# Down projection of a feed-forward block in seven block products over pairs of batches

## The chip, the cores and the metric

The kernel runs on one core of a Trainium2 chip. The metric is device time in microseconds (us). The times given for the kernel before are three runs of it; a profile is one further execution. All arithmetic is in float32.

In the text PE is the matrix engine, PEld its loading of the stationary operand, DVE the vector engine, ACT the scalar engine, POOL the GpSimd engine, and SP the engine that issues most of the transfers. A line such as L721 is a line of the kernel's source. The changed kernel is longer, so its lines are given with the statement they hold.

## The reference, cut to what matters

The input x has 8 batches of 128 tokens with 512 features. A cross attention with 32 heads of 128 comes first, then a feed-forward block (FFN) of 1376 inner features; each has a layer norm ahead of it and a residual around it.

```python
def ffn(x):                       # Wg, Wu: 1376 x 512; Wd: 512 x 1376
    gate = einsum('bsh,ih->bsi', x, Wg) * ag
    up   = einsum('bsh,ih->bsi', x, Wu) * au
    h    = silu(gate) * up        # 8 x 128 x 1376
    return einsum('bsi,hi->bsh', h, Wd) * ad    # ad: one factor for each of 512 outputs
x = x + xattn(layernorm(x), ctx, mask, ...)
x = x + ffn(layernorm(x))
```

The change concerns the last `einsum`, its factor `ad`, and the last sum. It also splits off the code that makes `h`.

## The kernel before

The contracted axis always lies on the 128 partitions. 1376 inner features make 11 slices (`NI`), the last with 96 rows. A float32 matmul of the program shows up as two matmul records, so a count of records is twice the count of products.

**Seven products.** Most of the projections multiply two-by-two blocks with seven block products for eight. Sums of blocks of one operand (`sums_a`: s1, s2, s4 and one in place) and of the other (`sums_b`: t1, t2, t4 and one in place) are made beforehand, and PSUM results are combined afterwards. `seven` drives one such group for the FFN: product 2, product 1, then 6, 7 and 4 accumulated on top of product 1's banks, and then 5 and 3. Between products, ACT copies a bank out (L236, L246) or DVE adds it to what is in SBUF (L241, L252). The matmul that accumulates on a bank waits until that copy has read it.

**The stages at the end.** (1) Attention output projection for a pair of batches `i` (L470), each followed by `residual` (L537), which adds the seven products to x1. Two of its additions run on POOL: L545 for the left half of one batch, and L548 for the right half. Their result is `x1[i]`. (2) `norm2` (L558) takes mean and variance of `x1[i]` on DVE (L148, L149), and scales it to `y` (L567). (3) `norm2_T` transposes `y` on PE (L153), and DVE and ACT copy the result into `h2` (L579, L580). For the last pair (i = 3) this has one PSUM bank, so the second batch's transposes wait until both copies of the first are done. (4) `last_slice(0)` multiplies the 96-row slice for the first 512 tokens (L655, names `gp` and `up`). These 512 tokens need nothing of pair 3. (5) Sums of token blocks, `T_h` (L668 to L671, one of them on POOL: L669). (6) Five iterations of the gate and up projection, two slices each (L690, name `mm_f`), with POOL making sums of weights (L194 to L197), and `gated` (L640 on ACT, L641 and L644 on DVE) turning two results into `act`. (7) The down projection (L721, name `dn`):

```python
for n, ic in enumerate([NI - 1, *range(NI - 1)]):
    nc.tensor.matmul(
        o, act[ic][:m, bass.ts(b, S)], wd[:m, ic, cols],
        start=(n == 0), stop=(n == NI - 1),
    )
nc.vector.tensor_tensor(r[:, cols], o, ad_sb[:, cols], ALU.mult)
nc.vector.tensor_tensor(r[:, cols], r[:, cols], x1[b // 2][:, b % 2, cols], ALU.add)
nc.sync.dma_start(out[b][:, cols], r[:, cols])
```

Batches 0 to 6 have 11 products of 512 columns, and batch 7 has 22 of 256 columns in two halves, so that only half of its result remains at the end. The weights `wd` are loaded on SP (L627, L629).

**Order.** The order of the instructions on each engine is settled when the program is built, and isn't quite that of the source. The build moves an instruction ahead of others that were written earlier where its operands seem due sooner. In the trace, for example, POOL makes the weight sums of the first FFN iteration (L194 to L197, from 925.47 us) before the additions L545 and L548 of pair 3 (932.33 and 934.98 us), which are written earlier. On the chip each engine then takes its instructions in that order, and each waits for what it needs.

**Buffers.** `work` holds small tiles by tag ("pb", "tt", "s", "aT", "pT"), and a new tile of a tag waits until the oldest tile of that tag is free. `acts` has 18 buffers of 4 KB a partition for `x1`, `h2`, `gate` and the like; `ps` has 7 PSUM banks with the tag "m", and one with the tag "tp".

Of the kernel before, what the change touches and what calls it, by code (L numbers as in the profile page):

```python
# [10 lines left out]
F32 = mybir.dt.float32  # L11
U8 = mybir.dt.uint8
AF = mybir.ActivationFunctionType
ALU = mybir.AluOpType
# [3 lines left out]
P = 128  # L18
# [8 lines left out]
def xattn_ffn_kernel(  # L27
# [19 lines left out]
    nc = tc.nc  # L47
    B, S, D = x.shape
    H = pbias.shape[0]
    INTER = wgT.shape[1]  # L50
    T = B * S
# [5 lines left out]
    NI = (INTER + P - 1) // P  # L57
# [3 lines left out]
    HW = GW // 2  # L61
    ADD, SUB = ALU.add, ALU.subtract

    def pools(stack):
        def pool(name, bufs=1, **kw):
            return stack.enter_context(tc.tile_pool(name=name, bufs=bufs, **kw))
        return pool

    pool = pools(ctx)
# [3 lines left out]
    acts = pool("acts", 18, reuse_waits="tile")  # L73
    work = pool("work", 2, side="right", reuse_waits="tile")
# [7 lines left out]
    ps_mm, ps_tp, ps = (pools(attn)(f"ps{n}", 2, space=PSUM) for n in ("mm", "tp", "at"))  # L82
# [55 lines left out]
    ad_sb = const.tile([P, D], F32, name="ad_sb")  # L138
# [53 lines left out]
    def sums_a(eng, a11, a12, a21, a22, s1, s2, s4):  # L192

        eng.tensor_tensor(s1, a21, a22, ADD)  # L194
        eng.tensor_tensor(s2, s1, a11, SUB)
        eng.tensor_tensor(a21, a11, a21, SUB)
        eng.tensor_tensor(s4, a12, s2, SUB)  # L197
        return {1: a11, 2: a12, 3: s4, 4: a22, 5: s1, 6: s2, 7: a21}
# [94 lines left out]
    def probabilities(g, b, qT, kT, pb):  # L293
        cols = bass.ts(b, S)
        n = f"{g}_{b}"
        s = work.tile([P, GH, S], F32, tag="s", name=f"s_{n}", bufs=3)
        nc.gpsimd.tensor_tensor(  # L297
            s, pb, mneg[:, b : b + 1, :].to_broadcast([P, GH, S]), ALU.add
        )
        sc = ps.tile([P, GH, S], F32, tag="sc", name=f"sc_{n}")  # L300
        for j in range(GH):
            nc.tensor.matmul(  # L302
                sc[:, j, :], qT[:, j, bass.ts(b % 2, S)], kT[j][:, cols], start=True, stop=True
            )
        nc.vector.tensor_tensor(s, sc, s, ALU.add)  # L305
        mx = small.tile([P, GH], F32, tag="mx", name=f"mx_{n}")
        nc.vector.tensor_reduce(mx, s, AX.X, ALU.max)
        nmx = small.tile([P, GH], F32, tag="nmx", name=f"nmx_{n}")
        nc.vector.tensor_scalar(nmx, mx, FLOOR, -1.0, ALU.max, ALU.mult)  # L309
        sm = small.tile([P, GH], F32, tag="sm", name=f"sm_{n}")  # L310
        for j in range(GH):
            nc.scalar.activation(  # L312
                s[:, j, :], s[:, j, :], AF.Exp,
                bias=nmx[:, j : j + 1], accum_out=sm[:, j : j + 1],
            )
        ri = small.tile([P, GH], F32, tag="ri", name=f"ri_{n}")
        nc.vector.tensor_scalar_max(ri, sm, TINY)
        nc.vector.reciprocal(ri, ri)
        nc.vector.tensor_tensor(
            s, s, ri.unsqueeze(2).to_broadcast([P, GH, S]), ALU.mult  # L320
        )
        return s
# [137 lines left out]
    def by_product(banks):  # L460
        return {n: banks[k // 2][:, k % 2, :] for k, n in enumerate((1, 2, 6, 7, 4, 5, 3))}
# [26 lines left out]
    todo = [(g, i) for g in range(NG) for i in range(B // 2)]  # L488
# [3 lines left out]
    for g in range(NG):  # L492
        kT, v = kvs.pop(g)
        pb = biases.pop(g)
# [16 lines left out]
        for b in range(B):  # L511
# [5 lines left out]
            p = probabilities(g, b, qT, kT, pb)  # L517
# [15 lines left out]
    ps = pool("psO", 7, space=PSUM, reuse_waits="tile")  # L533
# [48 lines left out]
    x1, ys, banks = [], [], first_banks  # L582
    for i in range(B // 2):
        last = i + 1 == B // 2
# [7 lines left out]
        m = by_product(banks)  # L592
        x1.append(acts.tile([P, 2, D], F32, tag="a", name=f"x1_{i}"))
        for k in range(2):
            b = 2 * i + k
# [11 lines left out]

    fw = pool("fw", 4, reuse_waits="tile")
    wdp = pool("wdp", reuse_waits="tile")
    actp = pool("act", NI, reuse_waits="tile")  # L610
    NP = NI // 2

    def load_gate_up(i, eng=nc.sync):
# [10 lines left out]
    def load_down():  # L624
        t = wdp.tile([P, NI, D], F32, tag="wd", name="wd")
        full = INTER // P
        nc.sync.dma_start(t[:, :full, :], wdT[: full * P, :].rearrange("(c p) n -> p c n", p=P))  # L627
        if INTER % P:
            nc.sync.dma_start(t[: INTER % P, full, :], wdT[full * P :, :])  # L629
        return t  # L630

    act = [actp.tile([P, T], F32, tag="act", name=f"act_{ic}") for ic in range(NI)]
    alone = load_gate_up(NP, nc.gpsimd)
    gate_up = [load_gate_up(0, nc.gpsimd)]
    residual(i, x1[i], m, banks)
    ys = norm2(i, x1[i])

    def gated(act, gate, up, ic, m, sg):

        nc.scalar.activation(sg, gate, AF.Sigmoid, scale=ag_sb[:m, ic : ic + 1])  # L640
        nc.vector.scalar_tensor_tensor(  # L641
            sg, gate, ag_sb[:m, ic : ic + 1], sg, ALU.mult, ALU.mult
        )
        nc.vector.scalar_tensor_tensor(  # L644
            act, up, au_sb[:m, ic : ic + 1], sg, ALU.mult, ALU.mult
        )

    def last_slice(th):

        ic, m = NI - 1, INTER - (NI - 1) * P  # L650
        o = []
        for w, nm in zip(alone, ("gp", "up")):
            o.append(ps.tile([P, 512], F32, tag="m", name=f"{nm}_{th}"))
            for c in range(DC):
                nc.tensor.matmul(  # L655
                    o[-1][:m], w[:, c, :m], h2[c // HC, th][:, c % HC, :],
                    start=(c == 0), stop=(c == DC - 1),
                )
        sg = work.tile([P, 512], F32, tag="pT", name=f"sg_{th}", bufs=4)
        gated(act[ic][:m, bass.ts(th, 512)], o[0][:m], o[1][:m], ic, m, sg[:m])  # L660

    last_slice(0)
    for y in ys:
        norm2_T(*y)
    t1, t2, t3, t4 = (
        acts.tile([P, HC, 512], F32, tag="a", name=f"T{n}_h2") for n in range(1, 5)
    )
# [7 lines left out]
    for i in range(NP):  # L675
        ws, gate = [], [acts.tile([P, T], F32, tag="a", name=f"gate_{i}_{r}") for r in range(2)]
        for nm, w in zip("gu", gate_up[i]):
            s = fw.tile([P, 3, HC, P], F32, tag="S", name=f"S_{nm}{i}")
            ws.append(sums_a(
                nc.gpsimd, w[:, :HC, :P], w[:, HC:, :P], w[:, :HC, P:], w[:, HC:, P:],  # L680
                s[:, 0], s[:, 1], s[:, 2],
            ))
        if i + 1 < NP:
            gate_up.append(load_gate_up(i + 1))
        if i == 0:
            wd = load_down()

        def product(n, t, out, first):
            for c in range(HC):
                nc.tensor.matmul(  # L690
                    out, ws[t][n][:, c, :], h2_t[n][:, c, :],
                    start=(first and c == 0), stop=(c == HC - 1), skip_group_check=True,
                )

        def part(r, c, t):
            return (gate[r - 1], act[2 * i + r - 1])[t][:, bass.ts(c - 1, 512)]

        for n, _ in enumerate(seven(f"f{i}", range(2), product, part, ps, "m")):
            if i == 0 and n == 3:
                last_slice(1)  # L700
            if 4 <= n < 12 and n % 2 == 0 and gatings:
                gatings.pop(0)()
        for r in range(2):
            ic = 2 * i + r
            sg = acts.tile([P, T], F32, tag="a", name=f"sg_{ic}")
            for cols in (bass.ts(0, 512), bass.ts(1, 512)):
                gatings.append(partial(
                    gated, act[ic][:, cols], gate[r][:, cols], act[ic][:, cols], ic, P, sg[:, cols]
                ))
    for gating in gatings:  # L710
        gating()

    for b in range(B):
        r = work.tile([P, D], F32, tag="aT", name=f"r_{b}")
        parts = 1 if b + 1 < B else 2
        for k in range(parts):
            cols = bass.ts(k, D // parts)
            o = ps.tile([P, D // parts], F32, tag="m", name=f"dn_{b}_{k}")
            for n, ic in enumerate([NI - 1, *range(NI - 1)]):
                m = min(P, INTER - ic * P)  # L720
                nc.tensor.matmul(  # L721
                    o, act[ic][:m, bass.ts(b, S)], wd[:m, ic, cols],
                    start=(n == 0), stop=(n == NI - 1),
                )
            nc.vector.tensor_tensor(r[:, cols], o, ad_sb[:, cols], ALU.mult)
            nc.vector.tensor_tensor(r[:, cols], r[:, cols], x1[b // 2][:, b % 2, cols], ALU.add)
            nc.sync.dma_start(out[b][:, cols], r[:, cols])


# [41 lines left out]
```

## Time and profile before

| what | value |
|---|---|
| three runs | 1152.23 us median, 1151.07 to 1153.02 |
| the profiled execution, its own time | 1152.01 us |
| its span in the trace | 1150.2 us, so 1.8 us lie around the span |
| mean granted clock of PE | 0.991 |
| PE busy | 1120.0 us, 97% of the span |
| DVE, ACT, POOL busy | 502.3, 318.1, 297.9 us |
| end of attention output projection | 934.2 us from the start of the span |
| FFN gate and up | 934.2 to 1070.7 us |
| down projection on PE | 1070.7 to 1146.5 us |
| last DVE instruction to end of span (the last store) | 1147.4 to 1150.2 us |

The profile has one row for a group of instructions with the same line, engine and shapes. It gives the count, the busy time of the group, the mean duration of one in ns, and the idle time of the engine just before them with what ended it. Matmuls overlap, so their mean duration is longer than their spacing; spacing comes from busy time over count. The timeline lists instructions in order of time with start and length; runs of the same kind are merged.

### The profile page before, as it was taken

Reading aid. Unit: us, or ns where it says so; the run is one execution under the profiler, and the core shown is the slowest. Engines: PE = TensorE matmul, PEld = TensorE weight load, DVE = VectorE, ACT = ScalarE, POOL = GpSimd, SP = SyncE. Lnnn points to the kernel's source line nnn. Section 1 sums busy time; section 2 is a strip of 40 time slices with the busy share of each in tenths; the row PEclk is TensorE's granted clock in tenths of the full one; section 3 lists DMA queues with packets and bytes.
Section 4 is the critical chain, followed back from the end, with each engine's and each line's share of the span. In section 5 each row is a group of like instructions: output and inputs, shape, how many; then the busy total and the mean of one; then the engine's idle time right before and its main releaser. Section 6 shows DMA issues by size and latency. Waiting matters only on the chain.

```text
span 1150.2 us, 12321 instructions
## 1 busy us (share of the span) xinstructions
PE 1120.0 (97%) x4286; PEld 731.4 (64%) x4286; DVE 502.3 (44%) x957; ACT 318.1 (28%) x899; POOL 297.9 (26%) x255
## 2 busy tenths in 40 slices
PE   6999999999999999999999999789999999999998
PEld 3564444445867777686958689678888864444445
DVE  4541111116555555555555557824433242434311
ACT  2521112223444344444344443301000022223000
POOL 5331221116333333333223315620000034220000
PEclk9999999999999999999999999899999999999999
DMA  9114432257555455555554347865232332110000
GB/s 284 41 37 149 175 114 110 110 197 259 175 166 175 151 186 174 168 182 183 179 173 152 129 139 218 275 192 171 78 104 65 109 128 73 36 37 1 18 29 28
DMA packets 117533, 154.38 MB, mean 134 GB/s; under 512 B 12032, under 2 KB 71680, under 8 KB 117472
## 3 DMA queue, kind: packets, MB, share of 16 engines
q1 hardware_dynamic: 114784, 149.93, 40.3%
q10 hardware_dynamic: 2192, 2.10, 0.6%
q0 software_dynamic: 496, 1.58, 0.4%
q8 instruction: 34, 0.56, 0.2%
q14 instruction: 27, 0.22, 0.1%
HBM read 101.14 MB, written 52.43 MB: 134 GB/s over the span
## 4 chain that ended last, share of the span: by engine, by line
PE 91%; DVE 4%; DMA 2%; ACT 1%; issue 1%; POOL 0%; SPq 0%; ACTq 0%; DVEq 0%
PE mm_q L262 17%; PE mm_v L280 16%; PE m L470 16%; PE mm_k L262 16%; PE mm_f L690 9%; PE dn L721 7%; PE sc L302 4%; PE av L358 4%; DMA wk<-in_wkT_dram 1%; DMA wo<-in_woT_dram 1%; PE tp L153 1%; PE up L655 1%; PE gp L655 1%; DVE sg L641 1%; ACT s L312 0%
## 5 line engine op out<-in xcount | busy, mean ns | idle before, releaser
L297 POOL TENSOR_TENSOR s<-pb,mneg 128x512 f32<-128x512 f32 x64 | 81.2, 1269 | 291.1 <-DVE tt L335 217.3
L262 PE MATMUL mm_k<-ctx_sb,wk 128*128 128x512 f32 x256 | 117.8, 604 | 7.2 <-DMA wk<-in_wkT_dram 4.4
L280 PE MATMUL mm_v<-wv,ctx_sb 128*128 128x256 f32 x512 | 115.9, 379 | 0.8 <-DMA wv<-in_wvT_dram 0.8
L262 PE MATMUL mm_q<-hT,wq 128*128 128x512 f32 x256 | 112.5, 592 | 0.0
L312 ACT ACTIVATE s<-s,nmx 128x128 f32<-128x128 f32 x256 | 99.5, 390 | 36.0 <-DVE nmx L309 36.0
L470 PE MATMUL m<-wo,a 128*128 128x256 f32 x400 | 101.5, 392 | 6.6 <-DMA a<-att 6.5
L280 PEld LDWEIGHTS mm_v<-wv,ctx_sb 128*128 128x128 f32 x512 | 95.1, 190 | 14.4 <-DMA wv<-in_wvT_dram 1.6
L363 ACT COPY aT<-av 128x512 f32<-128x512 f32 x64 | 37.5, 586 | 203.3 <-PE av L358 105.4
L262 PE MATMUL mm_k<-ctx_sb,S_k 128*128 128x512 f32 x192 | 88.3, 607 | 4.3 <-DVE k L241 3.9
L470 PEld LDWEIGHTS m<-wo,a 128*128 128x128 f32 x400 | 77.7, 197 | 18.0 <-DMA a<-att 6.8
L262 PEld LDWEIGHTS mm_q<-hT,wq 128*128 128x128 f32 x256 | 48.6, 190 | 60.8 <-issue 60.7
L280 PE MATMUL mm_v<-S_v,ctx_sb 128*128 128x256 f32 x384 | 86.6, 381 | 0.0
L262 PEld LDWEIGHTS mm_k<-ctx_sb,wk 128*128 128x128 f32 x256 | 47.2, 194 | 60.1 <-issue 45.5
L262 PE MATMUL mm_q<-hT,S_q 128*128 128x512 f32 x192 | 85.0, 592 | 0.0
L305 DVE TENSOR_TENSOR s<-sc,s 128x512 f32<-128x512 f32 x64 | 44.2, 690 | 86.8 <-PE sc L302 83.6
L280 PEld LDWEIGHTS mm_v<-S_v,ctx_sb 128*128 128x128 f32 x384 | 71.5, 190 | 11.0 <-DVE v L252 1.8
L302 PEld LDWEIGHTS sc<-k,q 128*128 128x128 f32 x512 | 67.3, 194 | 17.4 <-issue 13.4
L721 PE MATMUL dn<-wd,act 128*128 128x512 f32 (+3 forms) x198 | 75.8, 545 | 0.0
L252 DVE TENSOR_TENSOR q<-q,mm_q 128x512 f32<-128x512 f32 x32 | 22.0, 688 | 114.8 <-PE mm_q L262 114.8
L302 PE MATMUL sc<-k,q 128*128 128x128 f32 x512 | 68.1, 277 | 2.0 <-DMA q<-queries 1.9
L358 PE MATMUL av<-pT,v 128*128 128x128 f32 x512 | 68.1, 277 | 0.0
L262 PEld LDWEIGHTS mm_k<-ctx_sb,S_k 128*128 128x128 f32 x192 | 35.4, 192 | 49.3 <-issue 35.7
(156 smaller groups left out, 1492.1 us busy)
## 6 DMA issues: line engine op xcount, KB each, us to landing
queries<-q SPq DMA_DIRECT2D x32, 512.0 KB, 3.8
q<-queries SPq DMA_DIRECT2D x32, 512.0 KB, 4.4
turned<-tt SPq DMA_DIRECT2D x64, 256.0 KB, 2.1
pT<-turned SPq DMA_DIRECT2D x256, 64.0 KB, 2.4
att<-aT SPq DMA_DIRECT2D x64, 256.0 KB, 2.3
a<-att SPq DMA_DIRECT2D x32, 512.0 KB, 3.5
wq<-in_wqT_dram SPq DMA_DIRECT2D x8, 1024.0 KB, 5.5
wk<-in_wkT_dram SPq DMA_DIRECT2D x7, 1024.0 KB, 6.1
```

What stands on the lines that cost most here:

```text
L262: nc.tensor.matmul(out, w[i][:, c, bass.ts(t, P)], src[i][:, c, :], start=(first and c == 0), stop=(c == HC - 1), skip_group_check=True,)
L280: nc.tensor.matmul(out[:, bass.ts(k, HW)], src[i][:, c, bass.ts(2 * t + k, S)], w[i][:, c, :], start=(first and k == 0 and c == 0), stop=( ...
L297: nc.gpsimd.tensor_tensor(s, pb, mneg[:, b : b + 1, :].to_broadcast([P, GH, S]), ALU.add)
L302: nc.tensor.matmul(sc[:, j, :], qT[:, j, bass.ts(b % 2, S)], kT[j][:, cols], start=True, stop=True)
L305: nc.vector.tensor_tensor(s, sc, s, ALU.add)
L312: nc.scalar.activation(s[:, j, :], s[:, j, :], AF.Exp, bias=nmx[:, j : j + 1], accum_out=sm[:, j : j + 1],)
L358: nc.tensor.matmul(av[:, j, :], v[b // 2][:, b % 2, bass.ts(j, P)], pT[:, :, j, :], start=True, stop=True,)
L363: nc.scalar.copy(aT, av)
L470: nc.tensor.matmul(m[n], sa[n][:, c, :], wo_t[g][n][:, c, :], start=(g == order[0] and c == 0 and k % 2 == 0), stop=(g == order[-1] and c ...
L655: nc.tensor.matmul(o[-1][:m], w[:, c, :m], h2[c // HC, th][:, c % HC, :], start=(c == 0), stop=(c == DC - 1),)
L690: nc.tensor.matmul(out, ws[t][n][:, c, :], h2_t[n][:, c, :], start=(first and c == 0), stop=(c == HC - 1), skip_group_check=True,)
L721: nc.tensor.matmul(o, act[ic][:m, bass.ts(b, S)], wd[:m, ic, cols], start=(n == 0), stop=(n == NI - 1),)
```

## The change

The down projection becomes seven block products. Batches b and b + 4 form the two row blocks, even and odd slices of the inner features the two inner blocks, and the two halves of the 512 outputs the two column blocks. The first ten slices make five pairs. The eleventh slice of 96 rows is added as four plain products of 256 columns (`LAST`). `wd` is multiplied by `ad` in place, and combined, by instructions on POOL (`weigh_down`): 11 multiplications of 512 columns and 20 sums of 256 columns. The sums lie in tiles of the tags "pb", "tt", "s" and "aT". In the source they are spread over iterations 1 to 3 of the gate and up projection. The sums of activations are made on DVE (`a_sums`). `act` becomes two tiles with five slices each, and one for the last slice, in place of eleven. `gated` takes its scratch tile from the tag "pT" in pieces of 512 columns, in place of `acts`. The results are added into `x1` in place (`down_out`), and stored from there.

```diff
@@ -607,7 +607,7 @@
 
     fw = pool("fw", 4, reuse_waits="tile")
     wdp = pool("wdp", reuse_waits="tile")
-    actp = pool("act", NI, reuse_waits="tile")
+    actp = pool("act", reuse_waits="tile")
     NP = NI // 2
 
     def load_gate_up(i, eng=nc.sync):
@@ -629,14 +629,45 @@
             nc.sync.dma_start(t[: INTER % P, full, :], wdT[full * P :, :])
         return t
 
-    act = [actp.tile([P, T], F32, tag="act", name=f"act_{ic}") for ic in range(NI)]
+    act_even, act_odd = (
+        actp.tile([P, NP, T], F32, tag=f"act{k}", name=f"act_{k}") for k in range(2)
+    )
+    act_rest = actp.tile([P, T], F32, tag="act2", name="act_2")
+    act = [(act_odd if ic % 2 else act_even)[:, ic // 2, :] for ic in range(NI - 1)] + [act_rest]
+
+    t_tags = [("pb", 2), ("pb", 2), ("tt", 2), ("tt", 2), ("s", 3), ("s", 3), ("s", 3), ("aT", 2)]
+    wd_t = {}
+
+    def weigh_down(wd):
+        tiles = [
+            work.tile([P, 2, HW], F32, tag=tag, name=f"T_d{k}", bufs=n)
+            for k, (tag, n) in enumerate(t_tags)
+        ]
+        spare = iter([t[:, h] for t in tiles for h in range(2)])
+        for n in range(1, 8):
+            wd_t[n] = []
+        for ic in range(NI):
+            m = min(P, INTER - ic * P)
+            yield partial(nc.gpsimd.tensor_tensor, wd[:m, ic], wd[:m, ic], ad_sb[:m], ALU.mult)
+            if ic % 2:
+                b11, b12 = wd[:, ic - 1, :HW], wd[:, ic - 1, HW:]
+                b21, b22 = wd[:, ic, :HW], wd[:, ic, HW:]
+                t1, t2, t4 = next(spare), next(spare), next(spare)
+                for n, t in enumerate((b11, b21, b22, t4, t1, t2, b12)):
+                    wd_t[n + 1].append(t)
+                yield partial(nc.gpsimd.tensor_tensor, t1, b12, b11, SUB)
+                yield partial(nc.gpsimd.tensor_tensor, t2, b22, t1, SUB)
+                yield partial(nc.gpsimd.tensor_tensor, b12, b22, b12, SUB)
+                yield partial(nc.gpsimd.tensor_tensor, t4, b21, t2, SUB)
+
     alone = load_gate_up(NP, nc.gpsimd)
     gate_up = [load_gate_up(0, nc.gpsimd)]
     residual(i, x1[i], m, banks)
     ys = norm2(i, x1[i])
 
-    def gated(act, gate, up, ic, m, sg):
-
+    def gated(act, gate, up, ic, m):
+
+        sg = work.tile([P, 512], F32, tag="pT", name=f"sg_{ic}", bufs=4)[:m]
         nc.scalar.activation(sg, gate, AF.Sigmoid, scale=ag_sb[:m, ic : ic + 1])
         nc.vector.scalar_tensor_tensor(
             sg, gate, ag_sb[:m, ic : ic + 1], sg, ALU.mult, ALU.mult
@@ -656,8 +687,7 @@
                     o[-1][:m], w[:, c, :m], h2[c // HC, th][:, c % HC, :],
                     start=(c == 0), stop=(c == DC - 1),
                 )
-        sg = work.tile([P, 512], F32, tag="pT", name=f"sg_{th}", bufs=4)
-        gated(act[ic][:m, bass.ts(th, 512)], o[0][:m], o[1][:m], ic, m, sg[:m])
+        gated(act[ic][:m, bass.ts(th, 512)], o[0][:m], o[1][:m], ic, m)
 
     last_slice(0)
     for y in ys:
@@ -684,6 +714,7 @@
             gate_up.append(load_gate_up(i + 1))
         if i == 0:
             wd = load_down()
+            down_sums = list(weigh_down(wd))
 
         def product(n, t, out, first):
             for c in range(HC):
@@ -700,31 +731,105 @@
                 last_slice(1)
             if 4 <= n < 12 and n % 2 == 0 and gatings:
                 gatings.pop(0)()
+            if 0 < i < NP - 1 and down_sums:
+                down_sums.pop(0)()
         for r in range(2):
             ic = 2 * i + r
-            sg = acts.tile([P, T], F32, tag="a", name=f"sg_{ic}")
             for cols in (bass.ts(0, 512), bass.ts(1, 512)):
                 gatings.append(partial(
-                    gated, act[ic][:, cols], gate[r][:, cols], act[ic][:, cols], ic, P, sg[:, cols]
+                    gated, act[ic][:, cols], gate[r][:, cols], act[ic][:, cols], ic, P
                 ))
     for gating in gatings:
         gating()
 
-    for b in range(B):
-        r = work.tile([P, D], F32, tag="aT", name=f"r_{b}")
-        parts = 1 if b + 1 < B else 2
-        for k in range(parts):
-            cols = bass.ts(k, D // parts)
-            o = ps.tile([P, D // parts], F32, tag="m", name=f"dn_{b}_{k}")
-            for n, ic in enumerate([NI - 1, *range(NI - 1)]):
-                m = min(P, INTER - ic * P)
-                nc.tensor.matmul(
-                    o, act[ic][:m, bass.ts(b, S)], wd[:m, ic, cols],
-                    start=(n == 0), stop=(n == NI - 1),
-                )
-            nc.vector.tensor_tensor(r[:, cols], o, ad_sb[:, cols], ALU.mult)
-            nc.vector.tensor_tensor(r[:, cols], r[:, cols], x1[b // 2][:, b % 2, cols], ALU.add)
-            nc.sync.dma_start(out[b][:, cols], r[:, cols])
+
+
+
+    HB = B // 2
+    act_last, w_last = act[NI - 1], wd[:, NI - 1]
+    m_last = INTER - (NI - 1) * P
+
+    def a_sums(b, parts):
+
+        s = [acts.tile([P, NP, S], F32, tag="a", name=f"S{k}_d{b}") for k in range(3)]
+        up, dn = bass.ts(b, S), bass.ts(b + HB, S)
+        for sl in parts:
+            sums_a(
+                nc.vector, act_even[:, sl, up], act_odd[:, sl, up],
+                act_even[:, sl, dn], act_odd[:, sl, dn], *(t[:, sl, :] for t in s),
+            )
+        return {
+            1: act_even[:, :, up], 2: act_odd[:, :, up], 3: s[2], 4: act_odd[:, :, dn],
+            5: s[0], 6: s[1], 7: act_even[:, :, dn],
+        }
+
+    LAST = {2: (0, 0), 3: (0, 1), 4: (1, 0), 8: (1, 1)}
+    ORDER = (2, 1, 6, 7, 4, 5, 8, 3)
+
+    def down(b, sa, last):
+
+        names = [(2, 1), (6, 7), (4, 5)] + ([(8,), (3,)] if last else [(8, 3)])
+        m = {}
+        for k, ns in enumerate(names):
+            tag = "tp" if k == 3 and b % 2 else "m"
+            t = ps.tile([P, 2, HW], F32, tag=tag, name=f"d{k}_{b}", bufs=1 if tag == "tp" else None)
+            for h, n in enumerate((5, 4) if ns == (4, 5) else ns):
+                m[n] = t[:, 1 - h if ns == (4, 5) else h, :], n == ns[0]
+            if ns == (4, 5):
+                both = t
+        todo = [(n, i) for n in ORDER for i in range(-1, NP)]
+        if b == 0:
+            todo.sort(key=lambda ni: ni[1])
+        todo = [(n, i) for n, i in todo if (n in LAST if i < 0 else n < 8)]
+        first_of = {}
+        for n, i in todo:
+            first_of.setdefault(n, i)
+        started = set()
+        for n, i in todo:
+            out, _ = m[n]
+            bank = next(k for k, ns in enumerate(names) if n in ns)
+            if i < 0:
+                r, c = LAST[n]
+                lhs = act_last[:m_last, bass.ts(b + r * HB, S)]
+                rhs = w_last[:m_last, bass.ts(c, HW)]
+            else:
+                lhs, rhs = sa[n][:, i, :], wd_t[n][i]
+            nc.tensor.matmul(
+                out, lhs, rhs, start=bank not in started,
+                stop=(i == NP - 1 or n == 8), skip_group_check=True,
+            )
+            started.add(bank)
+        return {n: o for n, (o, _) in m.items()}, both
+
+    def down_out(b, m, both, last):
+        r1, r2 = x1[b // 2][:, b % 2, :], x1[(b + HB) // 2][:, b % 2, :]
+        u = work.tile([P, 2, HW], F32, tag="pT", name=f"du_{b}", bufs=4)
+        w = work.tile([P, HW], F32, tag="pT", name=f"dw_{b}", bufs=4)
+        nc.scalar.copy(u[:, 0], m[1])
+        nc.vector.tensor_tensor(r1[:, :HW], r1[:, :HW], m[2], ADD)
+        nc.gpsimd.tensor_tensor(r1[:, :HW], r1[:, :HW], u[:, 0], ADD)
+        nc.vector.tensor_tensor(u[:, 1], u[:, 0], m[6], ADD)
+        nc.vector.tensor_tensor(w, u[:, 1], m[7], ADD)
+        nc.gpsimd.tensor_tensor(r1[:, HW:], r1[:, HW:], u[:, 1], ADD)
+        nc.vector.tensor_tensor(r2, r2, both[:].rearrange("p a n -> p (a n)"), ADD)
+        nc.vector.tensor_tensor(
+            r2.rearrange("p (a n) -> p a n", a=2), r2.rearrange("p (a n) -> p a n", a=2),
+            w.unsqueeze(1).to_broadcast([P, 2, HW]), ADD,
+        )
+        nc.vector.tensor_tensor(r1[:, HW:], r1[:, HW:], m[5], ADD)
+        nc.vector.tensor_tensor(r2[:, HW:], r2[:, HW:], m[8], ADD)
+        nc.sync.dma_start(out[b + HB], r2)
+        if last:
+            nc.sync.dma_start(out[b][:, :HW], r1[:, :HW])
+        nc.vector.tensor_tensor(r1[:, HW:], r1[:, HW:], m[3], ADD)
+        nc.sync.dma_start(*((out[b][:, HW:], r1[:, HW:]) if last else (out[b], r1)))
+
+    sa = a_sums(0, (slice(0, NP - 1), slice(NP - 1, NP)))
+    for b in range(HB):
+        coming = a_sums(b + 1, (slice(0, NP),)) if b + 1 < HB else None
+        last = b + 1 == HB
+        down_out(b, *down(b, sa, last), last)
+        sa = coming
 
 
 # ---- launch: one core; weights and context are laid out with the contracted axis first ----
```

`sums_a` is the function that the other stages use already: s1 = a21 + a22, s2 = s1 - a11, a21 = a11 - a21 in place, s4 = a12 - s2.

## What is predicted, and from what

> **What bounds the kernel now.** I read the page's busy times and its chain of waits first.
>
> ```profile
> PE 1120.0 (97%) x4286; PEld 731.4 (64%) x4286; DVE 502.3 (44%) x957; ACT 318.1 (28%) x899; POOL 297.9 (26%) x255
> PE 91%; DVE 4%; DMA 2%; ACT 1%; issue 1%; POOL 0%; SPq 0%; ACTq 0%; DVEq 0%
> ```
>
> PE is busy for 97% of the span and makes 91% of the chain. So a product less is time less, and anything that makes PE wait is time more. Next, the groups of the last stage by shape, and the chain's row of a stage with 256-column products.
>
> ```profile
> L721 PE MATMUL dn<-wd,act 128*128 128x512 f32 x140 | 61.2, 592 | 0.0
> L721 PE MATMUL dn<-wd,act 128*128 128x256 f32 x40 | 9.0, 379 | 0.0
> ```
>
> ```profile
> 855.09 47.05 PE m L470 x218
> ```
>
> Idle time is 0.0: this stage is bound by PE alone. In its 256-column form a record takes 47.05 / 218 = 0.2158 us, half of a 512-column record (0.43 us in the timeline). So smaller products lose nothing.
>
> Then the timelines of POOL, DVE and PE ahead of the FFN, where the added POOL work will stand.
>
> ```profile
> 930.49 0.73 POOL L197 TENSOR_TENSOR S_u<-wu,S_u 128x256 f32<-128x256 f32 x1
> 932.33 0.72 POOL L545 TENSOR_TENSOR x<-x,u 128x256 f32<-128x256 f32 x1 [1.11 <-DVE x L544]
> 934.98 1.11 POOL L548 TENSOR_TENSOR x<-x,u 128x256 f32<-128x256 f32 x1 [1.92 <-DVE x L547]
> ```
>
> ```profile
> 936.12 1.29 DVE L148 BATCH_NORM_STATS2 st<-x 128x6 f32<-128x512 f32 x2 [0.62 <-POOL x L548]
> ...
> 938.29 1.00 DVE L567 TENSOR_SCALAR y<-x,mv,rs 128x512 f32<-128x512 f32 x2
> ```
>
> ```profile
> 937.64 3.60 PE L655 MATMUL up<-h,wu 128*96 128x512 f32 x8
> 941.08 0.60 PE L153 MATMUL tp<-ident,y 128*128 128x128 f32 x4
> 941.51 1.88 PE L690 MATMUL mm_f<-h,wg 128*128 128x512 f32 x4
> 943.23 0.60 PE L153 MATMUL tp<-ident,y 128*128 128x128 f32 x4
> ```
>
> This is a chain: POOL L548, DVE statistics, y, PE transposes. The first y is there at 938.29 + 0.5 = 938.8 and PE comes to it at 941.08. The slack is 2.3 us.
>
> [...] The trace agrees: its order on POOL is that of the built program, row by row. [...] after 3.65 us of idle the granted clock was 0.51 from 774 to 777 us. [...] L548 took 1.11 us beside DVE's L550, L545 0.72 us. [...]
>
> **The change part by part.**
>
> *PE's products: -8.4 us.* Seven products of five slices, and four of the last slice, make 39 products a pair, 156 in all, 312 records of 256 columns: 312 x 0.2158 = 67.3 us. L721 takes 75.8 us now (1070.68 to 1146.46). Difference 8.4 us.
>
> *POOL's 31 new instructions: the heart of it.* The order of the changed program as built has them not in iterations 1 to 3, where the source emits them. They stand directly behind L197 of the first iteration: 18 ahead of L545, 7 between L545 and L548, 6 between L548 and L669. PE's order is as before up to the last stage, the transposes of pair 3 behind `up`. So they are on the path. Their prices, from the timeline of POOL:
>
> ```profile
> 117.20 1.27 POOL L194 TENSOR_TENSOR S_q<-wq 128x512 f32<-128x512 f32 x1 [18.96 <-PE mm_q L262]
> 118.56 1.27 POOL L195 TENSOR_TENSOR S_q<-S_q,wq 128x512 f32<-128x512 f32 x1
> 119.78 1.27 POOL L196 TENSOR_TENSOR wq<-wq 128x512 f32<-128x512 f32 x1
> 121.00 1.27 POOL L197 TENSOR_TENSOR S_q<-wq,S_q 128x512 f32<-128x512 f32 x1
> ```
>
> Start to start it is 1.22 us, and 1.36 us where the next waits for this result. Rows of 256 columns have 0.68 and 0.80 us (925.47 to 926.27 to 926.96). The multiplication isn't shown; I take the same price, since it too reads two SBUF operands.
> - The first can start at 931.2 behind L197. Its weights landed at 915.46 + 13.6 = 929.1 us, and SP's order is unchanged up to the stores.
> - Ahead of L545: 7 of 512 and 11 of 256, with four and two of them waited for: 16.8 us (bounds 16.0 and 18.3). Some 0.4 us [...]. L545 starts at 948.4, not 932.3.
> - L545 and the next seven (4 of 512, 3 of 256): 7.9 us. L548 runs 956.3 to 957.0; it ended at 936.1. That is 20.9 us late.
> - y: 938.8 + 20.9 = 959.7. PE, done with `up` at 941.1, waits 18.6 us.
> - The second transposes wait for the copies L579 and L580. DVE now has the two instructions of `gated` for the last slice ahead of L579. They wait for ACT's table load and sigmoid behind the statistics; before, PE's `up` came later than these. y + 1.3 us of sigmoid, 2 x 0.7 us on DVE, 0.4 us for each copy: 963.2, where they stood at 943.2. So the lateness is 20.0 us.
> - Clock. After the wait at 771.9 us, 12 records took 775.45 to 780.73, 5.3 us for 2.6 us of work. Here about 5 us at half clock; part lies within the wait for the copies. I take 1.2 us (bounds 0 and 2.7).
>
> Sum: +21.2 us. From there PE had no wait before that could take it up: product 6 of iteration 0 comes 12.5 us behind the second transposes, its sums 5.6 us behind them, and both shift together. The 6 rows behind L548 end before L669's inputs are there. Weight loads of iteration 1 follow PE and shift with it.
>
> *`gated` in pieces: -0.6 us (bounds -1.0 and +1.0).* PE waits 1.0 us in all for L241 now, because four gatings stand ahead of it. In the built order they stand earlier, and one sigmoid and one multiplication stand between the two L241. By the durations (0.69, 0.72, 0.75, 0.69 us) the second ends 0.3 us ahead of need.
>
> *Sums of activations, DVE: 0.* The last sums for the first pair end about 6.9 us into the last stage; they are needed 4 x 0.43 + 28 x 0.43 = 13.8 us in. If that cover were gone, up to 2 us. The pairs' results (8 DVE, 2 POOL and 1 ACT instruction, under 5 us) lie beside the next pair's 16.8 us.
>
> *End: 0 (bounds -0.5 and +0.7).* Behind the last product one addition of 0.42 us instead of two; but a store of 256 KB is issued just ahead of the last one.
>
> Sum: -8.4 + 21.2 - 0.6 = **+12.2 us**. Against its span, 1162.4; with 1.8 us around it 1164.2. The profiled execution is 0.2 us below the median, so 1164.4.
>
> **The rivals.**
> - *A, worse: DVE's new order in iterations 0 to 4.* If ACT has a copy (0.59 us) ahead of the sigmoid, or POOL's sums lengthen the multiplications (L641 took 2.08 us for two beside POOL, 1.42 otherwise), the second L241 comes late and product 6 waits. Up to 1 us in each of five: about 1169. Against it: 0.3 us of spare. 0.11.
> - *B, milder.* The multiplications or sums run a third faster than the nearest rows: 24 us become 16, and the lateness 13: 1156. Against it: every POOL row of that size in the trace has the price used. 0.08.
> - *C, not slower: POOL's rows are covered, and the eighth product is all that shows.* It is decided by the time of the 25 rows ahead of L548. With the 2.3 us of slack and POOL's own 3 us of idle, break-even is at 12 to 14 us, some 0.5 us a row, against 24.0 us by the rows. Fully covered it would be 1150.2 - 9.0 + 1.8 = 1143. For it: the source puts the rows where POOL is idle, and the addition of pair 3 could be earlier on the chip than its place says. Against: first in, first out. 0.05.
>
> That the product count doesn't fall is excluded by the built order (312 records).
>
> **How the numbers follow.** A measurement can tell about 0.2% from no change, 2.3 us. My forecast has 0.76, with its own range 1161 to 1168. A, B and the forecast are slower: 0.95. C ends mostly faster, 0.04, and 0.01 within 0.2%. The range takes in the forecast's bounds and most of A: 1160 to 1169.5.
>
> **What would show it.** PE idle of about 18 us ahead of L153, released by DVE y, and DVE's statistics waiting some 20 us for POOL's L548; POOL rows of `wd` back to back from 931 us; a granted clock near 0.5 at 960 to 964 us; the last stage 67 us long. I would be wrong if the transposes start before 950 us, if PE waits for L241 by over 3 us in all, or if the last stage has idle time.

## The result, and the profile after

| kernel | runs | median | range |
|---|---|---|---|
| before | 4 | 1151.65 us | 1150.24 to 1153.02 |
| changed | 4 | 1168.92 us | 1163.89 to 1171.39 |

The change makes the kernel slower: ratio 1.0145, 95% interval 1.0119 to 1.017. The prediction was slower, 1164.4 us with a range of 1160 to 1169.5. The median lies in the range, 4.5 us above the predicted time. The profiled execution is the lowest of the four, 1163.89 us with a span of 1162.1 us.

The page of the changed kernel, busy times and chain:

```profile
PE 1112.9 (96%) x4400; PEld 753.1 (65%) x4400; DVE 524.5 (45%) x991; ACT 320.8 (28%) x903; POOL 337.0 (29%) x294
PE 88%; DVE 5%; POOL 3%; DMA 2%; issue 1%; ACT 1%; ACTq 0%; SPq 0%; DVEq 0%
```

PE has less work (1112.9 us for 1120.0), yet the span is 11.9 us longer. POOL, which had 0% of the chain, has 3% now, and DVE 5% for 4%. So time went from work on PE to waiting for others. The timeline of POOL shows where (start, length, then what ended an idle time):

```profile
927.65 0.73 POOL L197 TENSOR_TENSOR S_u<-wu,S_u 128x256 f32<-128x256 f32 x1
928.33 2.50 POOL L735 TENSOR_TENSOR wd<-wd,ad_sb 128x512 f32<-128x512 f32 x2
...
944.19 0.73 POOL L735 TENSOR_TENSOR wd<-wd 128x256 f32<-128x256 f32 x1
944.87 0.73 POOL L545 TENSOR_TENSOR x<-x,u 128x256 f32<-128x256 f32 x1
945.55 3.71 POOL L735 TENSOR_TENSOR wd<-wd,ad_sb 128x512 f32<-128x512 f32 x3
...
952.47 0.72 POOL L548 TENSOR_TENSOR x<-x,u 128x256 f32<-128x256 f32 x1
```

L735 is `weigh_down`. Its rows run without a gap from 928.33 us until after L548, and L545 and L548 come where the queue has put them. All 282 `TENSOR_TENSOR` instructions of POOL in this trace, and all 243 in that of the kernel before, start in the order of the built program; so do DVE's 991 and 957 instructions. DVE and PE then show the consequence; the number in brackets is idle time and its releaser:

```profile
953.23 1.29 DVE L148 BATCH_NORM_STATS2 st<-x 128x6 f32<-128x512 f32 x2 [19.93 <-POOL x L548]
...
955.89 1.60 DVE L567 TENSOR_SCALAR y<-x,mv,rs 128x512 f32<-128x512 f32 x2
```

```profile
934.32 3.60 PE L686 MATMUL up<-h,wu 128*96 128x512 f32 x8
957.19 1.09 PE L153 MATMUL tp<-ident,y 128*128 128x128 f32 x4 [19.27 <-DVE y L567]
958.07 3.62 PE L721 MATMUL mm_f<-h,wg 128*128 128x512 f32 x4
961.48 0.84 PE L153 MATMUL tp<-ident,y 128*128 128x128 f32 x4
```

PE waits 19.27 us. The four records at 958.07 us then take 3.62 us, where they took 1.88 us before: that is half clock (granted clock 0.50 from 942 to 961 us). Last, the group and the chain's row of the last stage:

```profile
L797 PE MATMUL d<-wd,act 128*128 128x256 f32 x120 | 28.5, 379 | 0.0
L797 PE MATMUL d<-T_d,S_d 128*128 128x256 f32 x80 | 19.9, 379 | 0.0
```

```profile
1091.40 67.39 PE d L797 x312
```

The stage has no idle time and takes 67.4 us for 75.8. So the seven products gave the 8.4 us that was reckoned, and the wait of 19.27 us ahead of the FFN took more than twice as much.

**One measure for all the kernels below.** The same code ahead of the FFN ends at different times in different executions: `gp`, the first product of the FFN, begins between 927.99 and 936.72 us in the twelve traces of this study. So I split each trace from `gp` on, into A (start of `gp` to start of the second transposes), B (from there to the first product of the last stage) and C (to the end of the span). These are free of what varies ahead of `gp`.

| kernel | A | B | C | sum | against before |
|---|---|---|---|---|---|
| before | 9.02 | 127.45 | 79.52 | 215.99 | |
| changed | 30.60 | 129.76 | 70.86 | 231.22 | +15.2 |
| e1, the changed again | 29.89 | 129.04 | 70.83 | 229.76 | +13.8 |
| e2, rows later | 9.02 | 141.16 | 70.83 | 221.01 | +5.0 |
| e3, pair 3's additions on DVE | 10.79 | 137.15 | 70.78 | 218.72 | +2.7 |
| e4, before with the rows | 29.90 | 128.08 | 79.07 | 237.05 | +21.1 |
| e5, old gating | 30.44 | 127.61 | 70.87 | 228.92 | +12.9 |
| e6, no multiplications | 16.44 | 128.97 | 70.87 | 216.28 | +0.3 |
| e7, nothing behind the rows | 10.88 | 128.44 | 70.83 | 210.15 | -5.8 |
| e8, e7 and old gating | 10.50 | 127.50 | 70.91 | 208.91 | -7.1 |
| e9, before with e7's moves | 9.02 | 127.47 | 79.57 | 216.06 | +0.1 |
| e10, e8 again | 10.66 | 127.52 | 70.90 | 209.08 | -6.9 |

The times of whole runs agree with this within their spread:

| kernel | median | range | ratio to before, 95% interval |
|---|---|---|---|
| e1 | 1166.04 us | 1165.43 to 1166.8 | 1.0128, 1.0113 to 1.0143 |
| e2 | 1156.21 us | 1151.63 to 1157.69 | 1.004, 1.003 to 1.0049 |
| e3 | 1154.61 us | 1152.91 to 1157.56 | 1.0033, 1.0019 to 1.0048 |
| e4 | 1172.14 us | 1171.34 to 1176.92 | 1.0195, 1.0171 to 1.0218 |
| e5 | 1166.07 us | 1163.3 to 1167.8 | 1.0121, 1.0104 to 1.0138 |
| e6 | 1151.45 us | 1149.1 to 1154.76 | 0.9999, 0.9988 to 1.0009 |
| e7 | 1145.69 us | 1142.67 to 1150.25 | 0.9953, 0.9936 to 0.9969 |
| e8 | 1143.78 us | 1138.71 to 1148.24 | 0.9944, 0.9925 to 0.9963 |
| e9 | 1152.01 us | 1149.31 to 1155.58 | 0.9999, 0.999 to 1.0008 |
| e10 | 1145.5 us | 1141.42 to 1149.2 | 0.9935, 0.9913 to 0.9956 |

The kernel before had medians of 1151.24 us beside e1 to e4, 1151.19 beside e5 to e8, and 1151.98 beside e9 and e10; each of these three groups ran on a chip of its own. The ratio given is not the quotient of two medians, and differs from it by up to 0.1%.

### The profile page after: what moved, and what is told of

Its sections match the earlier page's. It is cut to its first block, busy times and chain, and to the rows that moved or that the text cites. A ratio compares the mean times of both kernels' runs of the same rounds, so it can differ in the third digit from the quotient of the medians.

```text
span 1162.1 us, 12634 instructions
## 1 busy us (share of the span) xinstructions
PE 1112.9 (96%) x4400; PEld 753.1 (65%) x4400; DVE 524.5 (45%) x991; ACT 320.8 (28%) x903; POOL 337.0 (29%) x294
## 4 chain that ended last, share of the span: by engine, by line
PE 88%; DVE 5%; POOL 3%; DMA 2%; issue 1%; ACT 1%; ACTq 0%; SPq 0%; DVEq 0%
PE mm_q L262 17%; PE mm_v L280 16%; PE m L470 15%; PE mm_k L262 15%; PE mm_f L721 8%; PE d L797 6%; PE av L358 5%; PE sc L302 5%; POOL wd L735 1%; DVE sg L672 1%; DMA wg<-in_wgT_dram 1%; PE tp L153 1%; DMA wv<-in_wvT_dram 1%; POOL T_d L735 1%; DVE act L675 1%
## 5 line engine op out<-in xcount | busy, mean ns | idle before, releaser
L302 PE MATMUL sc<-k,q 128*128 128x128 f32 x512 | 67.3, 275 | 2.7 <-DMA q<-queries 1.8
L358 PE MATMUL av<-pT,v 128*128 128x128 f32 x512 | 67.4, 275 | 0.0
L262 PEld LDWEIGHTS mm_q<-hT,S_q 128*128 128x128 f32 x192 | 36.5, 190 | 45.9 <-issue 45.9
```

Source lines behind the costliest of these rows:

```text
L262: nc.tensor.matmul(out, w[i][:, c, bass.ts(t, P)], src[i][:, c, :], start=(first and c == 0), stop=(c == HC - 1), skip_group_check=True,)
L302: nc.tensor.matmul(sc[:, j, :], qT[:, j, bass.ts(b % 2, S)], kT[j][:, cols], start=True, stop=True)
L358: nc.tensor.matmul(av[:, j, :], v[b // 2][:, b % 2, bass.ts(j, P)], pT[:, :, j, :], start=True, stop=True,)
```

## The experiments

My theory: the POOL rows, 25 of 31 of which the build puts ahead of L548 of pair 3, make PE wait, and nothing else of size is wrong with the change. The rivals: the new gating is a good part of it, the last stage falls short, or rows on POOL cost as much wherever they stand.

**e1: the changed kernel again.** No edit; it shares its runs of the kernel before with e2 to e4.

> The changed kernel as it is, once more, for a second trace: its four runs lay between 1163.9 and 1171.4 us, its one trace was of the fastest. Queue theory (POOL's rows of wd stand ahead of L545 and L548, PE waits for them): median 1164 to 1169, PE idle of 19 us ahead of the transposes L153 in this trace too, and any excess over 1163.9 lies elsewhere. Rival (the wait itself varies, by POOL's speed or by the length of the half clock): a slower trace shows it as a longer wait, or as a half clock over more than 5 us of work.

1166.04 us, and A, B, C as in the table: the same picture, with a wait of 18.57 us ahead of the transposes.

**e4: the kernel before, with the 31 rows.** This is the suspected cost without the gain. The output takes `ad` from the weights, as in the change; the sums are made and used by nothing. One sum of each pair, which the change makes in place, goes to a spare tile here, so that `wd` stays whole. In the trace 24 of the 31 rows run ahead of L548, where the change has 25.

```diff
+            down_sums = list(weigh_down(wd))
...
+            if 0 < i < NP - 1 and down_sums:
+                down_sums.pop(0)()
...
-            nc.vector.tensor_tensor(r[:, cols], o, ad_sb[:, cols], ALU.mult)
-            nc.vector.tensor_tensor(r[:, cols], r[:, cols], x1[b // 2][:, b % 2, cols], ALU.add)
+            nc.vector.tensor_tensor(r[:, cols], o, x1[b // 2][:, b % 2, cols], ALU.add)
```

> The kernel before with the 31 POOL rows added: wd is multiplied by ad on POOL (so L725 is dropped), and the 20 sums are made and not used. The eight products, act and gated stay as before. Queue theory: about 21 us of wait and half clock alone, nothing back from the products: 1171 to 1175 us, ratio 1.018. Rival (the new gatings or the last stage cost it): within 3 us of the kernel before.

1172.14 us. The timeline of PE in e4:

```profile
958.05 1.09 PE L153 MATMUL tp<-ident,y 128*128 128x128 f32 x4 [18.57 <-DVE y L567]
...
1090.43 75.78 PE L744 MATMUL dn<-wd,act 96*128 96x512 f32 x198
```

The rows alone cost 20.9 us by the medians and bring the same wait to a kernel that has the eight products still. A is e1's to 0.01 us; so close a match is chance, since L548 ends 0.6 us earlier after `gp` than in e1 and `y` (L567) takes 0.6 us longer. The step is shown: the wait comes from the rows, and from nothing in the new products or the gating.

**e2: the rows later.** The multiplications take a copy of `ad` that is made only once the last of iteration 0's gate results is there, so that the build can't put them early.

```diff
+        if i == 1:
+            nc.vector.tensor_scalar(one, gate[0][:, T - 1 : T], 0.0, 1.0, ALU.mult, ALU.add)
+            nc.vector.tensor_scalar(ad_late, ad_sb, one, None, ALU.mult)
...
-            yield partial(nc.gpsimd.tensor_tensor, wd[:m, ic], wd[:m, ic], ad_sb[:m], ALU.mult)
+            yield partial(nc.gpsimd.tensor_tensor, wd[:m, ic], wd[:m, ic], ad_late[:m], ALU.mult)
```

> The 31 rows of wd are made to stand behind L699: they multiply by a copy of ad that DVE makes from a result of FFN iteration 0. Two small DVE instructions are added, nothing else is changed. Queue theory: no wait ahead of the transposes, the 8.4 us of the seven products remain, less 0 to 2 us in the FFN iterations: 1143 to 1146 us, ratio 0.992 to 0.995. Rival (the loss lies in the new order of gatings, in the last stage or in its start): it stays above 1158 us.

A miss: 1156.21 us. A is 9.02, as in the kernel before, so the first wait is gone; but B is 13.7 us longer. The timelines of PE and of DVE in e2 show why (the two tiles that the edit needs are left out above):

```profile
980.12 3.45 PE L726 MATMUL mm_f<-T_h,S_g 128*128 128x512 f32 x4 [3.16 <-DVE gate L241]
1013.34 3.75 PE L726 MATMUL mm_f<-T_h,S_g 128*128 128x512 f32 x4 [7.46 <-DVE gate L241]
```

```profile
998.82 7.44 DVE L672 SCALAR_TENSOR_TENSOR sg<-gate,ag_sb,sg 128x512 f32<-128x512 f32 x1 [0.79 <-ACT sg L671]
1006.18 0.68 DVE L252 TENSOR_TENSOR act<-act,mm_f 128x512 f32<-128x512 f32 x1
```

A multiplication of the gating, 0.75 us otherwise, took 7.44 us beside POOL's unbroken rows, and the L241 behind it came late; PE waited, and the four records behind the two waits took 3.45 and 3.75 us for 1.88 (granted clock 0.50 from 980 to 983 us). Ahead of the first of the two waits six multiplications took 8.8 us together, where 0.75 us each makes 4.5; the two instructions of the edit itself add 1.1 us there. So the place that the source gives the rows, iterations 1 to 3, isn't free either, at least in the order that this kernel got.

**e3: L545 and L548 of pair 3 on DVE.** The rows stay early, but the transposes no longer hang on POOL.

```diff
-        nc.gpsimd.tensor_tensor(r1[:, :HW], r1[:, :HW], u[:, 0], ADD)
+        (nc.vector if i == 3 else nc.gpsimd).tensor_tensor(r1[:, :HW], r1[:, :HW], u[:, 0], ADD)
...
-        nc.gpsimd.tensor_tensor(r1[:, HW:], r1[:, HW:], u[:, 1], ADD)
+        (nc.vector if i == 3 else nc.gpsimd).tensor_tensor(r1[:, HW:], r1[:, HW:], u[:, 1], ADD)
```

> The rows of wd stay where they are; the two additions of pair 3 behind them (L545, L548) go from POOL to DVE. Queue theory: the link is cut, so the transposes are on time (PE idle ahead of them under 2 us). L699, one token sum that product 7 of iteration 0 needs, still stands behind the 31 rows and comes late: 2 to 4 us of wait there, so 1145 to 1150 us. Rival (rows on POOL slow DVE's statistics [...]): still over 1158 us.

A miss of some 5 us: 1154.61 us. The wait ahead of the transposes is gone (0.20 us), but the next one in the queue took its place. The timeline of PE in e3:

```profile
960.00 1.88 PE L721 MATMUL mm_f<-T_h,S_u 128*128 128x512 f32 x4
967.63 3.78 PE L721 MATMUL mm_f<-T_h,wg 128*128 128x512 f32 x4 [5.75 <-POOL T_h L699]
971.20 2.82 PE L721 MATMUL mm_f<-T_h,wu 128*128 128x512 f32 x4
```

L699 is the token sum that POOL makes behind all 31 rows (L669 before). The expectation had named this sum, but put its wait at 2 to 4 us and left out the half clock behind it (granted clock 0.50 from 967 to 973 us). B is 8.7 us longer than in e7, where this wait is gone.

**e5: the old gating in the changed kernel.**

```diff
-        sg = work.tile([P, 512], F32, tag="pT", name=f"sg_{ic}", bufs=4)[:m]
...
+            sg = acts.tile([P, T], F32, tag="a", name=f"sg_{ic}")
...
-                    gated, act[ic][:, cols], gate[r][:, cols], act[ic][:, cols], ic, P
+                    gated, act[ic][:, cols], gate[r][:, cols], act[ic][:, cols], ic, P, sg[:, cols]
```

> The changed kernel with the gating as before it: sg from acts, one per slice. Nothing else changed; the 31 rows stay behind L197 of iteration 0. Theory: the gating in pieces costs about 1.0 us, since from the second transposes to the last stage e1 took 129.0 us and e4, which has the old gating and the same wait, 128.1 us; the pieces lie beside POOL's weight sums, and PE's weight loads then wait 1.0 us for S_u in each of three iterations. So 1165.0 against 1166.0 us of the changed kernel, these waits gone, and the wait of 18.6 us ahead of L153 unchanged. Rival 1 (my prediction): the pieces save 0.6 us, so 1166.6 here. Rival 2 (A of the prediction at its full size): they cost 3 us and more, so under 1163.

1166.07 us, with an interval of the ratio that overlaps e1's: as a time it decides nothing. The trace has 0.8 us less than e1, and no wait for S_u; rival 2 is out. e7 and e8 settle the size.

**e6: 14 rows for 25 ahead of L548.** The 11 multiplications are left out, so the output lacks the factor `ad`.

```diff
-            yield partial(nc.gpsimd.tensor_tensor, wd[:m, ic], wd[:m, ic], ad_sb[:m], ALU.mult)
```

> The changed kernel without the 11 multiplications of wd by ad (so the output lacks the factor ad). 14 rows of 256 columns stay ahead of L548, in place of 25 rows. Theory: the stall is the time of the rows ahead of L548 less some 2 us of slack. 11 rows ahead of L545 take 8.0 us from 931.4, L545 and three rows 2.8 us, so L548 ends near 943 and not 956.3 us; the transposes move 13.3 us up, PE waits 5.3 us and not 18.6, and the half clock stays. 1166.0 - 13.3 = 1152.7, between 1151 and 1155. Rival 1: it is not the rows' number but that they stand there at all (one wait for the load of wd or for a buffer): 1164 to 1166. Rival 2: below some length the stall is covered and the clock stays whole: 1144 to 1147.

1151.45 us. The timeline of PE in e6:

```profile
948.87 1.09 PE L153 MATMUL tp<-ident,y 128*128 128x128 f32 x4 [5.12 <-DVE y L567]
949.75 3.62 PE L720 MATMUL mm_f<-h,wg 128*128 128x512 f32 x4
```

The wait is 5.12 us, 5.3 expected. It follows the time of the rows. The four records at half clock cost the same 3.62 us behind 5.12 us of wait as behind 19.27.

**e7: nothing that PE needs stands behind the rows.** e3's edit, and L699 on DVE.

```diff
-    nc.gpsimd.tensor_tensor(t3, h2[1, 1], h2[0, 1], SUB)
+    nc.vector.tensor_tensor(t3, h2[1, 1], h2[0, 1], SUB)
```

> As e3 (L545 and L548 of pair 3 on DVE), and the token sum L699 on DVE too, so that nothing PE waits for in the first iteration stands behind the 31 rows. Theory: e3 lost 5.75 us to the wait for L699 and some 1.9 us to the half clock behind it; both go. DVE's chain of L698, L699, L700, L701, L241 grows by 1.5 to 3 us and has 4.6 us. 1154.6 - 7.6 = 1147.0, between 1145.5 and 1149, about 4 us under the kernel before. Rival 1: the wait only changes its place (L241 or L700 late behind L699 [...]): 1151 to 1155. Rival 2: the down projection's gain is lost elsewhere whatever stands on POOL: 1152 and more.

1145.69 us, 1147.0 expected: 0.5% faster than the kernel before, with the rows where the build puts them. The wait ahead of the transposes is 0.29 us, and there is none for L699's sum.

**e8: e7 with e5's edit.**

> As e7, with the gating as before the change. Theory: the same 1.0 us as between e5 and the changed kernel: 1146.0, between 1144.5 and 1148, about 0.5% under the kernel before. Rival: without the stall the gating in one piece stands ahead of L241 as it did before, and nothing is won: 1147 to 1148.

1143.78 us, a little under the range given. The medians of e7 and e8 differ by 1.9 us, with ranges that overlap; the two traces differ by 0.94 us in B, the same as e1 and e4 (0.96). The timelines of PE in e7, then in e8, over one iteration:

```profile
978.56 1.96 PE L721 MATMUL mm_f<-T_h,S_g 128*128 128x512 f32 x4 [0.22 <-DVE gate L241]
980.70 1.95 PE L721 MATMUL mm_f<-T_h,S_u 128*128 128x512 f32 x4 [0.18 <-DVE act L241]
...
1003.47 1.10 PE L721 MATMUL mm_f<-T_h,S_g 128*128 128x512 f32 x2 [0.22 <-DVE gate L241]
```

```profile
975.53 1.95 PE L721 MATMUL mm_f<-T_h,S_g 128*128 128x512 f32 x4 [0.33 <-DVE gate L241]
977.32 1.88 PE L721 MATMUL mm_f<-T_h,S_u 128*128 128x512 f32 x4
...
1000.12 1.10 PE L721 MATMUL mm_f<-T_h,S_g 128*128 128x512 f32 x2 [0.33 <-DVE gate L241]
```

An iteration takes 24.91 us in e7 and 24.59 in e8. In e7 PE's stream is broken twice, once for each L241, and in e8 once. A break costs some 0.2 us more than the idle time in brackets: the four records at 978.56 us are 2.14 us from start to start with the next, of which 0.18 is idle and 1.72 their time in an unbroken stream. The timeline of DVE in e7 has the cause:

```profile
998.11 2.35 DVE L675 SCALAR_TENSOR_TENSOR act<-act,au_sb,sg 128x512 f32<-128x512 f32 x2
1000.39 1.21 DVE L672 SCALAR_TENSOR_TENSOR sg<-gate,ag_sb,sg 128x512 f32<-128x512 f32 x1
1001.63 1.09 DVE L675 SCALAR_TENSOR_TENSOR act<-act,au_sb,sg 128x512 f32<-128x512 f32 x1
1002.65 0.67 DVE L241 TENSOR_TENSOR gate<-gate,mm_f 128x512 f32<-128x512 f32 x1
```

In pieces, the gating lies beside POOL's weight sums, its multiplications stretch from 0.75 to 1.1 us and more, and L241 comes later.

**e9: the kernel before with e7's three moves; e10: e8 again.**

> The kernel before the change with only the three moves of e7: L545 and L548 of pair 3 and the token sum L699 (there L669) on DVE. It tells whether e8's gain comes from the projection or from these moves. Theory: in the kernel before nothing waited for POOL here (slack of 2.3 us ahead of the transposes, no wait for the token sums), so the moves change nothing: 1151.2, between 1150.5 and 1152.5; e8 then stands 7 to 8.7 us under it, near the 8.4 us of the products. Rival: the moves themselves shorten the path (POOL's additions of 0.7 to 1.1 us become 0.42 to 0.95 us on DVE): 1148 to 1149.5, and the projection is worth only some 4 to 5 us.

> e8 again, beside e9 on the same chip: the changed projection with nothing behind its rows and the gating as before. Expected 1143.8, between 1142 and 1145.5; from the start of gp to the end of the span 208.9 us, as in e8, against 216.0 us in the kernel before. Rival: e8's figure was helped by a quick first part of the program (its gp began at 928.0 us, 934.2 in the kernel before): then 1146 to 1148.

e9 is at 1152.01 us, ratio 0.9999: the moves change nothing by themselves. e10 is at 1145.5 us, ratio 0.9935, although its `gp` began at 936.52 us, as late as almost any here. Its sum from `gp` on is e8's to 0.2 us. The profiled executions of the two, 1138.71 and 1147.39 us, are 8.7 us apart, and 8.5 us of this lie ahead of `gp`; whether a quick first part helped e8's median too, as the rival has it, isn't shown. The gain of 6.5 to 7.4 us belongs to the projection, once nothing that PE needs stands behind its rows. Of the 8.6 us that C is shorter, A takes 1.5 to 1.6 back: the second transposes wait 1.22 us for a copy (L580), which the kernel before doesn't have. DVE's work ahead of that copy is longer beside the rows (L567 takes 1.96 us in e8 and 1.00 in e9); that this is the whole reason isn't shown. This version beats both kernels.

## Why the prediction was right, and where it was off

All five marks that it named are in the profile above: the idle PE released by `y`, DVE's statistics waiting for L548, the rows back to back, half clock behind the wait (to 962 us; `gp` began 3.3 us earlier than before), and 67 us without idle time at the end. Lateness below is against `gp`, in e1, beside the prediction's own numbers. One more line bears on it, from the timeline of ACT in the first trace, the last copy of the first transposes:

```profile
959.65 0.37 ACT L580 COPY h<-tp 128x256 f32<-128x256 f32 x1 [2.00 <-DVE h L579]
```

- *POOL's rows.* L545 starts 15.8 us late (16.1 predicted), L548 ends 20.4 us late (20.9). The price of a row held, for the multiplications too (1.22 us start to start). Of the 16.1 us, 0.4 was an estimate of what DVE's work beside the rows would add, from 1.11 us of L548 beside L550 against 0.72 of L545 in the trace of the kernel before; in e1 the row beside L550 took 1.19 us, 0.73 to 0.75 elsewhere ahead of L548. The wait was 18.57 us in e1 and 19.27 in the first trace (18.6). That it is these rows and no other part is shown by e4.
- *Second transposes and clock: the sum was right, its split was not.* A is 20.9 us longer (20.0 predicted), and e4 has 0.6 us more of half clock behind it: 21.5 us for 21.2. I had 1.4 us for the wait for the copies and 1.2 for the clock. In e1 the first transposes and the four records behind them take 4.29 us from start to start, 2.15 before, so with the 0.6 us the clock alone cost 2.7 us. The copies cost nothing at half clock, since they were done before PE came to need them. In the first trace the last of them ends at 960.02 us, and the second transposes start at 961.48. At full clock the copies do hold PE up, by 1.21 us in e7. That my two terms add up to what the clock cost alone is luck.
- *PE's products.* 67.39 us in the chain, 67.3 predicted. C is 8.7 us shorter in all.
- *End.* Predicted 0, and C has 0.3 us more of gain than the products. e4 has 0.45 us of this with eight products and one DVE instruction less at the end, so the second addition's absence is worth about its 0.42 us, and the second store costs little.
- ***`gated` in pieces* is the step that failed.** Predicted -0.6 us (bounds -1.0 and +1.0); measured +0.95, between e1 and e4 and between e7 and e8 alike. I placed the gatings by the build's order and gave each the duration it has alone. But in the new order they lie beside POOL's weight sums, and both are stretched: in an iteration of e7, six of POOL's eight sums take 1.06 to 1.29 us in place of 0.73, in e8 one. This is the mechanism of rival A, at a fifth of its size. PE's waits for L241 are six and 1.2 us in all in e1, three and 1.0 us before; each break costs more than its idle time, as e7 has shown. In the first trace they are 2.3 us, 1.1 more than in e1, so there the cost is about 2 us, above my bound.

By these steps e1 is 21.5 + 0.95 - 8.7 = +13.8 us, where I had +12.2: nearly all the difference is the gating. (The steps are read from the traces of e1 and e4, so that they add up is no proof of its own.) The first trace has 1.5 us more than e1: 1.1 in waits for L241, 0.7 in the wait for `y`, and 0.4 less of half clock. The medians have +14.8 (e1) and +17.3 us (first runs). What they have beyond it isn't explained: nothing here traces the runs that had no profile, and what lies ahead of `gp` varies by 8.7 us among the traces.

*Rival C's break-even was too high.* I put it at 12 to 14 us of rows ahead of L548. e6, within 0.2% of the kernel before, has 10.2 us of them (933.91 to 944.79 us, less L545). Its wait is only 5.12 us, but the half clock behind it costs 2.7 us all the same, and the gating's 0.95 us was to be paid too.

My expectations of e2 and e3 failed in the same place, at what comes when the first wait is gone. In e2 I put at most 2 us on the FFN iterations, but with DVE's gating beside the rows they grew by 13.7; in e3 I named the token sum behind the rows, but with 2 to 4 us of wait where it was 5.75, and without the half clock.

## What to carry to other kernels

Work put on an idle engine made PE wait for 18.57 us where instructions of the path stood behind it in that engine's queue (e1), and for 0.29 us ahead of the same transposes where none did (e7): look up its place in the built order, not in the source, and list every later instruction there whose result PE takes. Moving those few instructions to another engine (three here) can be cheaper than moving the new work. Before adding two-input work on POOL, look at what DVE does at that time, since each stretched the other here: DVE's multiplications took 1.1 to 7.44 us for 0.75, and POOL's sums of 256 columns 1.1 to 1.3 us for 0.73.

## What the runs showed of the hardware

**In these traces a longer wait didn't make the half clock behind it dearer.** The table has PE's waits of over 1 us from `gp` on, in five of the traces. "Lost" is how much longer the work behind the wait took than at full clock, from start to start, until the records follow at 0.43 us again.

| wait | where | four 512-column records | lost |
|---|---|---|---|
| 1.22 us | e3, second transposes | 1.88 us | 0.1 us |
| 3.16 us | e2 | 3.45 us | 1.6 us |
| 5.12 us | e6 | 3.62 us | 2.7 us |
| 5.75 us | e3 | 3.78 us | 2.8 us |
| 7.46 us | e2 | 3.75 us | 2.0 us |
| 18.57 us | e1 | 3.62 us | 2.8 us |
| 19.27 us | changed | 3.62 us | 2.4 us |

From 3.16 us on, the loss is 1.6 to 2.8 us and doesn't grow with the wait. The granted clock was 0.50 behind e2's 3.16 us (980 to 983 us) and e3's 5.75 us (967 to 973 us), and in the changed kernel from 942 us, within the wait, to 961 us. For e1, e6 and e2's 7.46 us the half clock is read from the times of the records alone. What lies between 1.22 and 3.16 us isn't shown.

**In e2 one DVE multiplication lasted over nine POOL instructions in a row.** The multiplication at 998.82 us took 7.44 us, 0.75 otherwise, and ended at 1006.26 us. Beside it POOL ran nine instructions back to back, from 998.45 to 1005.70 us. The timeline of POOL in e2, its last part:

```profile
1004.31 0.71 POOL L740 TENSOR_TENSOR T_d<-wd,T_d 128x256 f32<-128x256 f32 x1
1004.99 0.71 POOL L194 TENSOR_TENSOR S_g<-wg 128x256 f32<-128x256 f32 x1
1005.79 1.06 POOL L195 TENSOR_TENSOR S_g<-S_g,wg 128x256 f32<-128x256 f32 x1
```

Up to 1004.99 us the instructions of 256 columns follow at 0.68 us; from there to L195, which needs L194's result, it is 0.80 us, and L195 takes 1.06 us itself, L196 behind it 0.72. In e6 DVE's L550 took 3.39 us, 0.68 before, and there too the first such gap, 0.81 us from 939.43, stands ahead of its end at 940.71 us. Whether the gaps have to do with it isn't shown: no run was made for it, and in e1 L550 ended after 1.75 us, beside rows that follow at 1.22 us without a gap. What ended the long stretches stays open.
